# Routing the last token tile by column halves, with a centred router, in a fused perceiver and mixture-of-experts kernel

## The chip, the cores and the metric

The kernel runs on one core of one Trainium2 chip. The metric is the device time of one execution in microseconds (us). Four engines compute: TensorE (PE, matrix products; its weight loads are listed as PEld), VectorE (DVE), ScalarE (ACT) and GpSimd (POOL). SyncE (SP) only issues transfers. Each engine works through its own instructions in order and waits on semaphores that the others raise.

## The reference

Everything is float32, and 512 tokens (8 x 64) of width 512 pass through three blocks, each with a residual. A cross attention over 1601 context rows and a linear attention with its MLP come first. The third block, a mixture of eight experts, is where the change lies:

```python
x = x + _L0_xattn_ref(_layernorm(x), ctx_1024, W, b)
x = x + _L0_attn_ref(_layernorm(x), ...)          # ends with + gelu(h2 @ w1 + b1) @ w2 + b2
m = _layernorm(x).reshape(-1, 512)                # 512 tokens
router_logits = m @ w_router                      # 512 x 8
top_w, top_i = top_k(router_logits, 2)
top_w = softmax(top_w)
for ei in range(8):
    out = out + gating[:, ei:ei+1] * ((silu(m @ w0[ei]) * (m @ w1[ei])) @ wo[ei])
x = x + out
```

This layernorm has no scale or shift of its own. So a logit is (x - mean) @ w_router divided by the token's standard deviation.

## The kernel before, in words

**Tiles.** The 512 tokens are NT = 4 tiles of 128. The width of 512 is KC = 4 chunks of 128. The instructions of each engine stand in the order in which the code writes them (a manual schedule), and waits are put in from the data flow. PSUM is eight banks: four under the tag `mm` and four under `acc`, each handed out in turn.

**End of the MLP.** `mlp_out(t, f, hid)` (L808) adds the product of hidden chunk f with `w2` to the bank `acc[t]`. The last HELD = 8 of the 16 hidden chunks are held back, and `last_chunks(t, part)` plays them tile by tile. A float32 product is two passes of TensorE, so a profile counts two instructions for each. `finish(t)` then adds the bank to the residual `xs` on DVE (L844), takes the mean and variance (L846, L848), the square root on ACT (L850), the reciprocal (L851), and writes the normalized tile `mn` (L852). ACT's queue stores `mn` to DRAM (L855), POOL's queue stores `xs` to the output (L856).

**Routing of a tile**, placed between the last chunks of the next tile:

- `turn_m(t)` transposes `mn` on PE (L867) and ACT copies the result to `m_t` (L869).
- `route(t)` multiplies with the router on PE (L875), copies the logits (L879), takes the two largest and their places (L880, L882), casts the places to floats as `chosen` (L883), and forms `hot` and `member` (L884, L890).
- `rank_tile(t)` counts on PE how many earlier tokens chose each expert (L904 with `members`, L905 with `member`); DVE makes `rank` (L906) and the one-hot matrix of the places in expert 0's list (L910).
- `first_rows(t)` (L915) multiplies `mn` with that matrix into one bank: the transposed rows of expert 0's first 128 tokens, gathered without going through DRAM.
- `count_tile(t)` updates `members` (L894, L896). `tabulate(t)` (L929 to L944) computes where each token goes in a table in DRAM, and POOL scatters two columns there with indirect transfers.

After the last tile, `xgT_first` is copied out of the bank (L975), the counts per expert are made (L982, L984) and so are the gating weights: L987, an exponential on ACT (L988), L990 to L997, and a store on ACT's queue (L998). POOL reads the table back as `late` (L1000).

**Experts.** `whole_tile` runs an expert's first 128 tokens: four `up` products (L1097), Silu on ACT (L1060), a product on DVE (L1062), a transpose on PE (`ht`, L1068), and the `y` products (L1105). Expert 0 reads `xgT_first`. The other experts' rows are fetched by indirect transfers through `late` (L1033) and transposed (L1051). An expert with 129 to 160 tokens runs `group` too (L1135 on), and one with over 160 runs `big_tile`s of 128 rows at the end. The buffers of this part reuse the memory of the part before it, so some of its first instructions also wait for the old part's transfers.

**Weights** come through a ring of twelve 1 MB buffers, issued by SP (L192) in a fixed order, each as soon as its buffer is free.

Of the kernel before, what the change touches and what calls it, by code (L numbers as in the profile page):

```python
# [15 lines left out]
F32 = mybir.dt.float32  # L16
AF = mybir.ActivationFunctionType
# [29 lines left out]
def perceiver_kernel(  # L47
# [189 lines left out]
    for e in range(NE):  # L237
# [16 lines left out]
    slot = const.tile([P, P], F32, name="slot")  # L254
    nc.gpsimd.iota(
        slot, pattern=[[1, P]], base=1, channel_multiplier=0, allow_small_or_imprecise_dtypes=True
    )
    token = const.tile([P, NT], F32, name="token")
    nc.gpsimd.iota(
# [142 lines left out]
    def late_loads():  # L402
        nc.sync.dma_start(out[B * S :, :], zero[:, :D])
        nc.sync.dma_start(table.rearrange("p k two -> p (k two)"), zero[:, : NE * NI * 2])
        nc.sync.dma_start(b2_bc, b2.partition_broadcast(P))
        for r in range(2):
            nc.sync.dma_start(proj2[r * DH : (r + 1) * DH, :], proj)
# [120 lines left out]
    def values(t, n):  # L528
# [5 lines left out]
            )  # L534
        nc.scalar.copy(v_sb[:, t, n * 512 : (n + 1) * 512], bank)

    for g in range(4):
        key_group(0, g)
    for g in range(2):
        key_group(1, g)  # L540
    for t in range(NT):
        turn_scores(t)
        if t == NT - 1:

            nc.scalar.activation(warm0, eps, AF.Sqrt)
        if t > 0:
            add_and_normalize(t - 1)
        weigh(t, 0)
        key_group(t + 1, 2)
        if 0 < t < NT - 1:  # L550
            turn_h(t - 1)
        weigh(t, 1)
        if t == NT - 1:
            turn_h(t - 1)
        key_group(t + 1, 3)
        weigh(t, 2)
        if t == NT - 3:
            late_loads()

        if t < NT - 2:  # L560
            key_group(t + 2, 0)
        else:
            values(t - 2, 0)
        turn_av(t)
        if t < NT - 2:
            key_group(t + 2, 1)
        else:
            values(t - 2, 1)
        attended(t)
# [269 lines left out]
    member = moe.tile(full, F32, name="member")  # L839
    members = moe.tile(full, F32, name="members")  # L840

    def finish(t):

        nc.vector.tensor_tensor(xs[:, t, :], acc[t], xs[:, t, :], ALU.add)  # L844
        st = small.tile([P, 6], F32, tag="st", name=f"st_m_{t}")
        nc.vector.bn_stats(st, xs[:, t, :])  # L846
        mv = small.tile([P, 2], F32, tag="mv1", name=f"mv_m_{t}")
        nc.vector.bn_aggr(mv, st)  # L848
        rstd = small.tile([P, 1], F32, tag="rstd1", name=f"rstd_m_{t}")
        nc.scalar.activation(rstd, mv[:, 1:2], AF.Sqrt, bias=eps)  # L850
        nc.vector.reciprocal(rstd, rstd)  # L851
        nc.vector.tensor_scalar(  # L852
            mn[:, t, :D], xs[:, t, :], mv[:, 0:1], rstd, ALU.subtract, ALU.mult
        )
        nc.scalar.dma_start(mn_dram[t * P : (t + 1) * P, :D], mn[:, t, :D])  # L855
        nc.gpsimd.dma_start(out[t * P : (t + 1) * P, :], xs[:, t, :])  # L856

# [1 line left out]
        for f in part:  # L859
            mlp_out(t, nf - HELD + f, hids[nf - HELD + f])  # L860

    m_ts = {}

    def turn_m(t):
        bank = mm_bank(f"tr_m_{t}")
        for c in range(KC):
            nc.tensor.transpose(bank[:, c * P : (c + 1) * P], mn[:, t, c * P : (c + 1) * P], ident)  # L867
        m_ts[t] = mlp2.tile([P, KC, P], F32, tag="mT", name=f"m_t_{t}")
        nc.scalar.copy(m_ts[t].rearrange("p c q -> p (c q)"), bank)  # L869

    def route(t):

        bank = mm_bank(f"router_{t}")
        for c in range(KC):
            nc.tensor.matmul(  # L875
                bank[:, :NE], m_ts[t][:, c, :], router[:, c, :], start=(c == 0), stop=(c == KC - 1)
            )
        logits = small.tile([P, NE], F32, tag="logits", name=f"logits_{t}")
        nc.vector.tensor_copy(logits, bank[:, :NE])  # L879
        nc.vector.max(out=top[:, t, :], in_=logits)  # L880
        where = small.tile([P, NE], mybir.dt.uint32, tag="where", name=f"where_{t}")
        nc.vector.max_index(out=where, in_max=top[:, t, :], in_values=logits)  # L882
        nc.vector.tensor_copy(chosen[:, t, :], where[:, :2])  # L883
        nc.vector.tensor_tensor(  # L884
            hot[:, t, :, :],
            enum[:, None, :].to_broadcast([P, 2, NE]),
            chosen[:, t, :, None].to_broadcast([P, 2, NE]),
            ALU.is_equal,
        )
        nc.vector.tensor_tensor(member[:, t, :], hot[:, t, 0, :], hot[:, t, 1, :], ALU.add)  # L890

    def count_tile(t):
        if t == 0:
            nc.vector.tensor_copy(members[:, 0, :], member[:, 0, :])  # L894
        else:
            nc.vector.tensor_tensor(members[:, t, :], members[:, t - 1, :], member[:, t, :], ALU.add)  # L896

    onehots = {}

    def rank_tile(t):  # L900

        bank = mm_bank(f"rank_{t}")
        if t > 0:
            nc.tensor.matmul(bank[:, :NE], ones, members[:, t - 1, :], start=True, stop=False)  # L904
        nc.tensor.matmul(bank[:, :NE], earlier, member[:, t, :], start=(t == 0), stop=True)  # L905
        nc.vector.scalar_tensor_tensor(  # L906
            rank[:, t, :], bank[:, :NE], 1.0, member[:, t, :], ALU.add, ALU.mult
        )
        onehots[t] = mlp2.tile([P, P], F32, tag="onehot", name=f"onehot_{t}")
        nc.vector.tensor_scalar(onehots[t], slot[:, :P], rank[:, t, 0:1], None, ALU.is_equal)  # L910

    def first_rows(t):

        for c in range(KC):
            nc.tensor.matmul(  # L915
                first_bank[:, c * P : (c + 1) * P],
                mn[:, t, c * P : (c + 1) * P],
                onehots[t],
                start=(t == 0 and c == 0),
                stop=(t == NT - 1),  # L920
                skip_group_check=True,
            )

    def tabulate(t):

# [26 lines left out]

    last_chunks(0, range(HELD))
    finish(0)
    first_bank = acc_bank("first_rows")
    for t in range(1, NT):

        last_chunks(t, range(0, 4))
        turn_m(t - 1)
        last_chunks(t, range(4, 5))  # L960
        route(t - 1)
        last_chunks(t, range(5, 7))
        rank_tile(t - 1)
        last_chunks(t, range(7, HELD))
        finish(t)
        first_rows(t - 1)
        if t > 1:
            tabulate(t - 2)
        count_tile(t - 1)
    turn_m(NT - 1)  # L970
    route(NT - 1)
    rank_tile(NT - 1)
    first_rows(NT - 1)
    xg_t0 = moe.tile([P, KC, P], F32, name="xgT_first")
    nc.scalar.copy(xg_t0.rearrange("p c q -> p (c q)"), first_bank)  # L975
    count_tile(NT - 1)
    for t in range(NT - 2, NT):
        tabulate(t)


    bank = mm_bank("counts")
    nc.tensor.matmul(bank[:, :NE], ones, members[:, NT - 1, :], start=True, stop=True)  # L982
    count = moe.tile([P, NE], F32, name="count")
    nc.vector.tensor_copy(count, bank[:, :NE])  # L984

    e2 = moe.tile([P, NT], F32, name="e2")
    nc.vector.tensor_tensor(e2, top[:, :, 1], top[:, :, 0], ALU.subtract)  # L987
    nc.scalar.activation(e2, e2, AF.Exp)  # L988
    r1 = moe.tile([P, NT], F32, name="r1")
    nc.vector.tensor_scalar_add(r1, e2, 1.0)  # L990
# [17 lines left out]
    if True:  # L1008
# [36 lines left out]
        def turn_tile(key, n=P):  # L1045

            xg = fetched[key]
            name = f"xgt_{key[0]}_{key[1]}"
            bank = (y_bank("w", name) if n == P else side_bank(1, name))
            for c in range(KC):  # L1050
                nc.tensor.transpose(  # L1051
                    bank[:, c * n : (c + 1) * n], xg[:n, c * P : (c + 1) * P], ident[:n, :n]
                )
            xg_t = moe2.tile([P, KC, n], F32, tag=f"xgT{n}", name=f"xgT_{key[0]}_{key[1]}")
            evacuate(xg_t.rearrange("p c q -> p (c q)"), bank[:, : KC * n])
            turned[key] = xg_t

        def gated(side, bank, name):
            act = moe2.tile([P, FQ], F32, tag=f"act{side}", name=f"act_{name}")
# [28 lines left out]
        def whole_tile(key, up_of, down_of, between=lambda k: None):  # L1088
# [5 lines left out]
            def up(q):  # L1094
                bank = side_bank(0, f"up_{nm}_{q}")
                for c in range(KC):
                    nc.tensor.matmul(  # L1097
                        bank, xg_t[:, c, :], up_of[q][:, c, :], start=(c == 0), stop=(c == KC - 1)
                    )
                return gated(0, bank, f"{nm}_{q}")  # L1100

# [25 lines left out]
        def group(e, up_of, down_of):  # L1127
# [5 lines left out]
            for c in range(KC):  # L1133
                for q in range(NQ):
                    nc.tensor.matmul(  # L1135
                        bank[q * R : (q + 1) * R, :],
                        xg_t[:, c, :],
                        up_of[q][:, c, :],
                        start=(c == 0),
                        stop=(c == KC - 1),  # L1140
                    )
# [17 lines left out]
        if True:  # L1159
# [135 lines left out]
                    [tiles["wo", n] for n in range(2)],  # L1295
                )

            turned[0, 0] = xg_t0
            for e in range(NE):

                def between(k, e=e):
# [126 lines left out]
```

## Time and profile before

| | us |
|---|---|
| three runs of the kernel before | 671.36, 673.45, 673.49 (median 673.45) |
| the profiled execution's own time | 672.11 |
| its span, first to last instruction | 670.4 |
| PE busy in the span | 627.2 (94%) |
| DVE, ACT, POOL busy | 175.5, 128.3, 61.6 |
| mean granted TensorE clock | 0.981 |

Times below are us from the start of the profiled span. A matmul's start is well placed; its end is modelled, so starts are compared with starts. "PEclk" is the share of full speed that the TensorE clock had.

### The profile page before, as it was taken

What the parts mean: (1) busy time and instruction counts of PE and PEld (TensorE: products, weight loads), DVE (VectorE), ACT (ScalarE), POOL (GpSimd) and SP (SyncE); (2) the same over time, 40 slices, a digit from 0 to 9 for tenths busy, and PEclk for the clock granted to TensorE, in tenths of its full rate; (3) what the DMA queues carried; (4) which work ended last, traced back from release to release, by engine and by line L of the source; (5) the groups of instructions that cost most, each with busy time, mean ns of one, the idle gap of its engine ahead of it and who ended that gap; (6) DMA issues with size and microseconds to landing.
All of it is one profiled execution on the core that took longest, in us unless ns stands there. A gap on an engine that the chain in (4) does not pass through costs nothing. (4 is left out here: it accounts for less than half of the span.)

```text
span 670.4 us, 6808 instructions
## 1 busy us (share of the span) xinstructions
PE 627.2 (94%) x2664; PEld 291.2 (43%) x2664; DVE 175.5 (26%) x419; ACT 128.3 (19%) x240; POOL 61.6 (9%) x81
## 2 busy tenths in 40 slices
PE   4998989799999999999999998899999899999993
PEld 3743434243444444454444455433444344334441
DVE  4011323122316888650000045311210111100100
ACT  2241222220132223031011211211111211111110
POOL 2000000000000000060000001340202202210000
PEclk9998999899999999999999999799999999999997
DMA  8999999999421203030213115029389576694611
GB/s 326 420 420 389 420 384 418 374 386 413 194 111 43 85 1 127 1 126 18 107 64 125 63 64 188 3 69 350 137 314 337 176 314 229 205 359 177 269 16 19
DMA packets 24224, 138.08 MB, mean 206 GB/s; under 512 B 4164, under 2 KB 4164, under 8 KB 11896
## 3 DMA queue, kind: packets, MB, share of 16 engines
q1 hardware_dynamic: 20056, 129.90, 49.7%
q0 software_dynamic: 3024, 6.58, 4.4%
q10 hardware_dynamic: 1104, 1.07, 0.5%
q8 instruction: 25, 0.41, 0.2%
q14 instruction: 15, 0.12, 0.1%
HBM read 132.56 MB, written 4.97 MB: 205 GB/s over the span
## 5 line engine op out<-in xcount | busy, mean ns | idle before, releaser
L1097 PE MATMUL up<-e_up,xgT 128*128 128x512 f32 x224 | 100.2, 595 | 1.2 <-PEq L1326 1.2
L1097 PEld LDWEIGHTS up<-e_up,xgT 128*128 128x128 f32 x224 | 40.9, 190 | 50.4 <-issue 50.4
L1105 PE MATMUL y<-e_wo,hidT 128*128 128x512 f32 x128 | 61.0, 599 | 0.0
L808 PE MATMUL mlp<-w,hid_sb 128*128 128x512 f32 x128 | 58.8, 597 | 0.0
L1062 DVE TENSOR_TENSOR mid<-up,act 128x256 f32<-128x256 f32 x35 | 14.9, 425 | 162.4 <-ACT act L1060 162.4
L472 PE MATMUL av<-ctx,eT 128*64 128x512 f32 x192 | 50.2, 636 | 7.3 <-DMA ctx<-in_ctx_dram 6.5
L787 PE MATMUL hid<-v_sb,w 128*128 128x512 f32 (+2 forms) x144 | 56.6, 545 | 0.0
L423 PE MATMUL sc<-ctxT,pw_t 128*64 128x401 f32 (+1 forms) x256 | 48.1, 501 | 0.6 <-DMA ctxT<-in_ctx_T_dram 0.6
L787 PEld LDWEIGHTS hid<-v_sb,w 128*128 128x128 f32 x144 | 26.2, 190 | 29.1 <-issue 27.3
L808 PEld LDWEIGHTS mlp<-w,hid_sb 128*128 128x128 f32 x128 | 23.4, 190 | 24.9 <-issue 24.9
L1060 ACT ACTIVATE act<-up 128x256 f32<-128x256 f32 x35 | 13.4, 384 | 104.5 <-PE up L1097 95.6
L1078 POOL DMA_INDIRECT out_dram<-y_sb,dst_late x11 | 16.8, 1530 | 160.9 <-ACTq L1326 103.7
L423 PEld LDWEIGHTS sc<-ctxT,pw_t 128*64 128x64 f32 x256 | 20.2, 136 | 26.0 <-issue 22.6
L802 POOL TENSOR_TENSOR xin<-xin,b_bc 128x512 f32<-128x512 f32 x4 | 5.1, 1269 | 283.4 <-DVE rstd_h L744 279.1
L1105 PEld LDWEIGHTS y<-e_wo,hidT 128*128 128x128 f32 x128 | 22.4, 190 | 19.5 <-issue 19.1
L472 PEld LDWEIGHTS av<-ctx,eT 128*64 128x64 f32 x192 | 15.2, 143 | 35.8 <-issue 24.3
L706 PE MATMUL wo<-wo,a_t 128*128 128x512 f32 x64 | 29.1, 600 | 0.5 <-DVE a_t L682 0.5
L595 PE MATMUL wk<-h_t,wk 128*128 128x512 f32 x64 | 29.5, 604 | 0.0
L595 PE MATMUL wq<-h_t,wq 128*128 128x512 f32 x64 | 29.4, 602 | 0.0
L532 PE MATMUL v<-wv,h_t 128*128 128x512 f32 x64 | 28.7, 597 | 0.6 <-DVE h_t L519 0.6
L680 DVE RECIPROCAL rden<-rden 128x512 f32<-128x512 f32 x8 | 26.8, 3353 | 0.3
L844 DVE TENSOR_TENSOR xs<-mlp,xs 128x512 f32<-128x512 f32 x4 | 2.8, 691 | 87.3 <-PE mlp L808 87.3
(229 smaller groups left out, 630.0 us busy)
## 6 DMA issues: line engine op xcount, KB each, us to landing
e_up<-in_L_ffn_up_dram SPq DMA_DIRECT2D x32, 1024.0 KB, 7.8
ctx<-in_ctx_dram SPq DMA_DIRECT2D x24, 1024.0 KB, 17.4
ctxT<-in_ctx_T_dram SPq DMA_DIRECT2D x24, 802.0 KB, 15.7
e_wo<-in_L_ffn_wo_dram SPq DMA_DIRECT2D x16, 1024.0 KB, 11.3
w<-in_L_attn_w_dram SPq DMA_DIRECT2D x8, 1024.0 KB, 10.9
ctxT<-in_ctx_T_dram SPq DMA_DIRECT2D x8, 796.0 KB, 16.7
big_up<-in_L_ffn_up_dram SPq DMA_DIRECT2D x4, 1024.0 KB, 7.9
wv<-in_L_attn_wv_dram SPq DMA_DIRECT2D x2, 1024.0 KB, 13.1
```

What stands on the lines that cost most here:

```text
L423: nc.tensor.matmul(sc[h * S : (h + 1) * S, :width], pw_t[:, c, (2 * t + h) * S : (2 * t + h + 1) * S], keys[h][:, c, :], start=(c == 0), s ...
L472: nc.tensor.matmul(av[h * S : (h + 1) * S, :], e_t[:, 4 * g + j, h * S : (h + 1) * S], rows[h][:, j, :], start=(g == 0 and j == 0), stop=F ...
L532: nc.tensor.matmul(bank, h_t[:, c, t * P : (t + 1) * P], wv_n[:, c, :], start=(c == 0), stop=(c == KC - 1))
L595: nc.tensor.matmul(bank, w[:, c, (j % 4) * P : (j % 4 + 1) * P], h_t[:, c, :], start=(c == 0), stop=(c == KC - 1),)
L680: nc.vector.reciprocal(rden, rden)
L706: nc.tensor.matmul(wo_banks[t], a_t[:, j, t * P : (t + 1) * P], wo_r[j // 4][:, j % 4, :], start=(j == 0), stop=(j == nj - 1),)
L787: nc.tensor.matmul(hid_banks[f][:, tokens], w[:, c, (f % 4) * P : (f % 4 + 1) * P], h2_t[:, c, tokens], start=(c == 0), stop=(c == KC - 1),)
L808: nc.tensor.matmul(acc[t], hid[:, t * P : (t + 1) * P], need("w2", f // 4)[:, f % 4, :], start=(f == 0), stop=(f == FF // P - 1),)
L1062: nc.vector.tensor_tensor(hid, bank[:, FQ:], act, ALU.mult)
L1078: nc.gpsimd.indirect_dma_start(out=out, out_offset=bass.IndirectOffsetOnAxis(ap=dst[:n, :], axis=0), in_=y_sb[:n, :], in_offset=None, boun ...
L1097: nc.tensor.matmul(bank, xg_t[:, c, :], up_of[q][:, c, :], start=(c == 0), stop=(c == KC - 1))
L1105: nc.tensor.matmul(y, h_t[:, j, :], w[:, 2 * (q % 2) + j, :], start=(q + j == 0), stop=(q + j == NQ))
```

## The change

The router's columns are centred once: the mean over the 512 rows is subtracted from each (`centre_router`, in the cross-attention stage). Then `xs @ router_c` is the logit times the token's standard deviation. The order of a token's logits is the same, so routing works on `xs` as it stands, ahead of the statistics. The difference of the two largest is multiplied by the reciprocal deviation later.

The last tile's held products are computed in two column halves, the second in a bank of its own. Tile 2's routing goes between the pieces of both halves, and so do the transposes and logits of the first half of tile 3. The gathering products `first_rows`, which had followed each tile, are all moved to the end, in portions that stand between the steps of the last tile's routing. They go to two banks that ACT and DVE copy out side by side. The logits are read from PSUM, and the places are compared without the cast in between. `rank` is off the one-hot's way, the counts are copied directly after the gathered rows, `tabulate` of tiles 0 and 1 comes one tile earlier, and tile 3's `mn` is made on ACT, its two stores issued after the counts. The diff, cut to its core:

```diff
+    router_c = const.tile([P, KC, NE], F32, name="router_c")
+    def centre_router():                       # called in the attention loop at t == NT - 3
+        bank = mm_bank("router_sums")
+        for c in range(KC):
+            nc.tensor.matmul(bank[:, :NE], ones, router[:, c, :], start=(c == 0), stop=(c == KC - 1))
+        nc.vector.scalar_tensor_tensor(
+            router_c, bank[:, None, :NE].to_broadcast([P, KC, NE]), -1.0 / D, router, ALU.mult, ALU.add)
...
-            nc.tensor.transpose(bank[:, c * P : (c + 1) * P], mn[:, t, c * P : (c + 1) * P], ident)
+            nc.tensor.transpose(bank[:, i * P : (i + 1) * P], xs[:, t, c * P : (c + 1) * P], ident)
...
-        nc.vector.tensor_copy(logits, bank[:, :NE])
+        logits = route_banks[t][:, :NE]
...
-        nc.vector.tensor_copy(chosen[:, t, :], where[:, :2])
...
+        onehots[t] = mlp2.tile([P, P], F32, tag="onehot", bufs=NT, name=f"onehot_{t}")
+        nc.vector.tensor_scalar(
+            onehots[t], slot0, bank[:, 0:1], member[:, t, 0:1], ALU.is_equal, ALU.mult
+        )
         nc.vector.scalar_tensor_tensor(
             rank[:, t, :], bank[:, :NE], 1.0, member[:, t, :], ALU.add, ALU.mult
         )
-        onehots[t] = mlp2.tile([P, P], F32, tag="onehot", name=f"onehot_{t}")
-        nc.vector.tensor_scalar(onehots[t], slot[:, :P], rank[:, t, 0:1], None, ALU.is_equal)
...
-    for t in range(1, NT):
-        last_chunks(t, range(0, 4))
+    for t in range(1, NT - 1):
+        last_chunks(t, range(0, 3))
         turn_m(t - 1)
-        last_chunks(t, range(4, 5))
-        route(t - 1)
+        rank_before(t - 1)
+        last_chunks(t, range(3, 5))
+        logits_of(t - 1)
+        choose(t - 1)
         last_chunks(t, range(5, 7))
         rank_tile(t - 1)
+        count_tile(t - 1)
         last_chunks(t, range(7, HELD))
         finish(t)
-        first_rows(t - 1)
-        if t > 1:
-            tabulate(t - 2)
-        count_tile(t - 1)
-    turn_m(NT - 1)
-    route(NT - 1)
-    rank_tile(NT - 1)
-    first_rows(NT - 1)
-    nc.scalar.copy(xg_t0.rearrange("p c q -> p (c q)"), first_bank)
-    count_tile(NT - 1)
+        tabulate(t - 1)
+    t = NT - 1
+    first_banks = [acc_bank(f"first_rows_{h}") for h in range(2)]
+    second_bank = acc_bank("mlp_second")
+    half_chunks(0, range(0, 5))              # 256 columns of the held products of tile 3
+    turn_m(t - 1)
+    rank_before(t - 1)
+    half_chunks(0, range(5, HELD))
+    for h in range(2):
+        nc.vector.tensor_tensor(xs[:, t, halves[h]], acc[t][:, halves[h]], xs[:, t, halves[h]], ALU.add)
+    logits_of(t - 1)
+    choose(t - 1)
+    half_chunks(1, range(0, 3))
+    turn_m(t, range(0, 2))
+    nc.vector.bn_stats(st[:, 0, :], xs[:, t, halves[0]])
+    half_chunks(1, range(3, 5))
+    rank_tile(t - 1)
+    count_tile(t - 1)
+    half_chunks(1, range(5, 7))
+    logits_of(t, range(0, 2))
+    rank_before(t)
+    half_chunks(1, range(7, HELD))
+    nc.vector.tensor_tensor(xs[:, t, halves[1]], second_bank[:, :HD], xs[:, t, halves[1]], ALU.add)
+    first_rows(4)
+    turn_m(t, range(2, KC))
+    nc.vector.bn_stats(st[:, 1, :], xs[:, t, halves[1]])
+    mv, rstd = moments(t, st)                # aggregate, square root on ACT, reciprocal
+    nc.vector.scalar_tensor_tensor(neg_mean, mv[:, 0:1], -1.0, rstd, ALU.mult, ALU.mult)
+    nc.scalar.activation(mn[:, t, :D], xs[:, t, :], AF.Identity, bias=neg_mean, scale=rstd)
+    first_rows(2)
+    logits_of(t, range(2, KC))
+    choose(t)
+    first_rows(5)
+    rank_tile(t)
+    first_rows(1)
+    count_tile(t)
+    first_rows(KC)
+    bank = mm_bank("counts")
+    nc.tensor.matmul(bank[:, :NE], ones, members[:, NT - 1, :], start=True, stop=True)
+    for h, copy in enumerate([nc.scalar.copy, nc.vector.tensor_copy]):
+        copy(xg_t0[h].rearrange("p c q -> p (c q)"), first_banks[h][:, : 2 * P])
+    nc.vector.tensor_copy(count, bank[:, :NE])
+    write(NT - 1)                            # the two stores of tile 3
     for t in range(NT - 2, NT):
         tabulate(t)
...
     nc.vector.tensor_tensor(e2, top[:, :, 1], top[:, :, 0], ALU.subtract)
+    nc.vector.tensor_tensor(e2, e2, rstds, ALU.mult)
     nc.scalar.activation(e2, e2, AF.Exp)
```

`first_rows(n)` now plays the next n of the sixteen products (tile t = i // 4, chunk c = i % 4). `rank_before(t)` is the L904 half of the ranking, and `logits_of` and `choose` are the two parts of `route`.

## The prediction

> **What bounds the kernel now.** I read the page first: PE is busy for 94% of the span, so only time that PE loses counts. The list of PE's waits after 424 us then shows none on a transfer, so what is gained before the experts should reach the end. The timeline of PE around the change shows the gap (columns: start, duration, engine, line, operation, count, idle time before and what ended it):
>
> ```profile
> 411.40 1.10 PE L808 MATMUL mlp<-w,hid_sb 128*128 128x512 f32 x2
> 412.34 1.05 PE L915 MATMUL first_rows<-onehot,mn 128*128 128x128 f32 x8
> 415.41 0.66 PE L867 MATMUL tr_m<-ident,mn 128*128 128x128 f32 x4 [2.02 <-DVE mn L852]
> 416.79 1.88 PE L875 MATMUL router<-col,m_t 128*128 128x8 f32 x8 [0.73 <-ACT m_t L869]
> 418.52 0.57 PE L904 MATMUL rank<-members,ones 128*128 128x8 f32 x2
> 420.02 0.59 PE L905 MATMUL rank<-member,earlier 128*128 128x8 f32 x2 [0.93 <-DVE member L890]
> 421.20 2.08 PE L915 MATMUL first_rows<-onehot,mn 128*128 128x128 f32 x8 [0.58 <-DVE onehot L910]
> 423.07 0.43 PE L982 MATMUL counts<-members,ones 128*128 128x8 f32 x2
> 423.95 1.22 PE L1097 MATMUL up<-e_up,xgT_first 128*128 128x512 f32 x1 [0.45 <-ACT xgT_first L975]
> ```
>
> After the last held product (next start 412.34) PE does little until `up` starts at 423.95: one tile's routing runs as a chain over four engines. The table by stretches shows the second loss (stretch, length, PE busy, granted clock, DMA share, GB/s):
>
> ```profile
> 413.35:416.76 3.41, 0.70 (x5) 1.00 0.88 293
> 416.76:420.17 3.41, 2.45 (x11) 0.50 0.45 171
> 420.17:423.59 3.42, 2.75 (x12) 0.50 0.02 3
> 423.59:427.00 3.41, 3.05 (x4) 0.50 0.01 0
> 427.00:430.41 3.41, 3.41 (x9) 1.00 0.08 5
> 635.21:638.62 3.41, 2.42 (x9) 1.00 0.01 2
> ```
>
> After a stretch in which PE was busy for 0.70 us the clock is halved for 10.2 us, into the first `up` products. Then ACT's timeline:
>
> ```profile
> 423.31 0.59 ACT L975 COPY xgT_first<-first_rows 128x512 f32<-128x512 f32 x1 [6.57 <-PE first_rows L915]
> 423.92 1.28 ACT L988 ACT_TABLE_LOAD   x1
> 425.21 0.20 ACT L988 ACTIVATE e<-e 128x4 f32<-128x4 f32 x1
> 426.52 0.38 ACTq L998 DMA_DIRECT2D mn_dram<-mn  x1
> 429.30 1.28 ACT L1060 ACT_TABLE_LOAD   x1 [3.88 <-PE up L1097]
> 430.59 0.38 ACT L1060 ACTIVATE act<-up 128x256 f32<-128x256 f32 x1
> ```
>
> In the built program the first Silu of expert 0 also waits for the landing of the gating store (L998), because the new buffers lie over the old `mn`. Here that is hidden: issued at 426.52, landed at 428.30 (its semaphore), and ACT waited for PE until 429.30.
>
> **The change part by part.** I count r from the start of the first PE instruction after tile 2's last product: 402.66 in this trace. In the kernel before, tile 3's products end at r 9.68, `up` starts at r 21.29, and the first transpose of expert 0 (`ht`) at 432.42, r 29.76.
>
> Rates at full clock, from PE's rows: a pass of 512 columns every 0.429 us, 256 columns every 0.216 (L368), 128 columns 0.112 (L915: 403.441 - 402.661 over 7), a router or rank pass 0.112, a transpose 0.108. PE to DVE takes about 0.2 us (409.20 to 409.41), a dependent step on DVE 0.2.
>
> *Tile 1.* `first_rows(0)` leaves the place after tile 1: 8 passes, 393.04 to 393.93, 0.89 us earlier for everything after. The work comes back at the end, below.
>
> *PE until the last held product.* Halves 0 to 4: 10 x 0.216 = 2.16; transposes 0.44; rank 0.22; three halves 1.30; router 0.92 (r 5.04); three 1.30; two transposes 0.22; two halves 0.86; rank 0.22; two 0.86; half of tile 3's logits 0.45; rank 0.22; the last 0.43. Sum: r 9.61. Does a wait come in? DVE has finished tile 2 and `tabulate(1)` at r 4.2 (402.93 to 406.9 here), adds the halves from 4.4 to 5.2, chooses from 5.28 to 6.14 (0.86; here 1.26 with the two copies L879 and L883, 0.2 each); the rank asks at 7.42. `members` is ready at 8.45, asked for at 8.95. So no, with 0.5 us to spare.
>
> *The tail.* DVE adds half 1, r 9.88 to 10.30. PE has `first_rows(4)`, to 10.51, transposes to 10.73, two products to 11.18. ACT copies 256 columns, 10.99 to 11.38. PE's logits 11.43 to 11.88. DVE chooses 12.15 to 13.01, behind the reciprocal and `neg_mean`, which wait for ACT's square root behind that copy. PE's five products end at 13.0; rank 13.05 to 13.27; one product; one-hot 13.45 to 13.74; the last four 13.78 to 14.68 (`mn` from ACT is ready at 12.74). Copies: ACT 14.43 to 14.80, DVE 14.88 to 15.29, counts to 15.49. The program lets `up` wait for that last copy, which holds the bank, not just for its data. So `up` starts at r 15.55: **5.74 us** earlier than 21.29.
>
> *First products to `ht`.* At full clock `up(0)` and `up(1)` take 16 x 0.429 = 6.87 instead of 8.47, so `ht` could come at r 22.4. But the gating chain is later: the counts are copied ahead of both `tabulate`s (1.23 us each, 421.14 to 422.37 to 423.60). From r 15.49: tables to 17.9, difference and the added product 0.35, exponential to 18.5, L990 to L997 to 19.57 (1.07 here), store issued 19.61 and landed 1.78 later, 21.4. Then the Silu table 1.28, Silu 0.38, the product 0.42, and steps between: `ht` at r 23.65. PE stalls 1.2 us where it had none; 29.76 - 23.65 = 6.11, of which 5.74 are counted: **0.37**. Behind the waiting Silu, ACT holds nothing that is due.
>
> [...] The row gives 1.28 us for the table load, and Silu starts 0.01 us after it (429.30 + 1.28, 430.59). [...]
>
> *The clock.* In this trace the clock fell after stretches with PE busy 0.70 us of 3.41 (and 1.03 at 58.36, 1.06 at 126.63), and held with 2.42. In the new tail PE idles about 1.3 us of 5.9, and in the stall 1.2, so it should hold. [...] The longest gap here is 2.02 us and it fell. [...] by the row, a poor window is enough, so the new tail is not out of danger. [...] the row gives the first rival.
>
> *Transfers.* Tile 3's `mn` store (ACT's queue) moves from 415.38 to about r 15, behind a copy; it delays the exponential's table load by 0.35, which still ends at 16.5, before it is needed. Its `xs` store on POOL's queue stays ahead of the scatters of tile 2, and those of tiles 0 and 1 run a tile earlier. So the scatters of tile 2 start when their places are ready, r 16.75, instead of at 424.43 (r 21.77), where the earlier scatter held them. From there to reading the table back takes 10.09 (to 434.52), so `late` comes 5.0 us earlier and PE's first use of a fetched row (444.89) about 6.1. The fetch was issued 6.45 us before that use and lands in 2.7 at best; a margin shrinks by 1.1, no stall. SP's last two loads of expert 1 wait for `w2` to be released, 2 us later at most, and are used after 457: nothing.
>
> *Centring.* Eight passes more, 0.9 us of PE near 106 us, plus a small product on DVE. In that stage PE later waits 2.65 us for context rows (128.98), which could absorb it all; if the loads are held by buffers that PE frees, it costs 0.9. I take **-0.4**. The extra iota on POOL (0.24 for its twin L255) lies at 3 us, ahead of idle time: nothing, and at most 0.24 without that.
>
> Sum: 0.89 + 5.74 + 0.37 - 0.4 = **6.6 us**. Against the profiled execution (672.11: span 670.4 and 1.7 around it) that is 665.5. The median of the runs is 673.45, which gives 666.9; I say 666.2, between.
>
> **The rivals.**
> - *The tail throttles* (15%). Small products and short gaps leave a window poor. Against it: busy shares near 80%. Price: the work after r 11, 3.5 us of PE time at most, doubled, and `up(0)` 1.7 slower of which 1.2 fills the stall. Gain 2.5 to 5: about 669.
> - *The gating store is late* (14%). PE's new stall lengthens one for one. The store of tile 3's `mn` took 4.1 us to land at 415.38 beside weight loads; [...] For it: the first `ht` now hangs on ACT and DVE. Against: DMA is at 0.01 to 0.08 there. Gain 4.3 to 5.2: 668.
> - *A router decision flips* (2%), which ends slower. The reference gives the experts 133, 104, 217, 159, 87, 132, 70 and 122 tokens, so expert 3 stands one token under 161. Rounding in the uncentred products would have to move one token to it; then its group (9.3 us, as the one from 581.06 to 590.33) becomes a second big tile, of about 24 us as the first (635.97 to about 660): +14 - 6.6, about 680. Against: the closest second and third logits differ by 0.0014 at a spread of 1.47.
> - *It does not do what it says* (4%): a bank or semaphore serializes the pieces, and the tail stays as long as it was: 672.
>
> **How the numbers follow.** The forecast has 65%, with its own range 664.5 to 668.5 (centring between 0 and -0.9, runs 2.1 us apart). With the two milder rivals the range is 664 to 670. A measurement of this kernel tells about 0.3% (2 us) from no change. Faster by more: the first three cases less 0.02 for their edges, 0.92; within: the last case and an edge, 0.05; slower: the flip and an edge, 0.03.
>
> **What would show it.** Right: no `first_rows` between tiles; PE's clock 1.00 through the tail; from tile 2's last product to `up` about 15.6 us; a stall of about 1.2 us before the first `ht`, ended by DVE's `mid` and behind it by the gating store. Wrong: half clock there, a stall over 3 us, PE waiting for fetched rows, or a fourth group or second big tile.

## The result, and the profile after

| | before | after |
|---|---|---|
| median of 5 runs, us | 673.45 (671.36 to 673.82) | 663.46 (662.06 to 665.04) |
| profiled execution's own time | 672.11 | 665.04 |
| its span | 670.4 | 663.3 |
| PE busy in the span | 627.2 | 624.8 |
| mean granted clock | 0.981 | 0.987 |

The ratio is 0.9856, with a 95% interval of 0.9835 to 0.9876. The change makes the kernel 10 us faster by these medians, and 7.1 us by the two traces. The profiled execution of before was among the faster of its runs, that of after the slowest of its five. In later runs the changed kernel had a median of 665.37 (662.93 to 665.68, 4 runs; ratio 0.9872, 0.9855 to 0.9889). All ten runs of it, in the order of size, are 662.06, 662.29, 662.93, 663.46, 663.69, 664.95, 665.04, 665.21, 665.54 and 665.68: a median of 664.3. The kernel before had medians of 673.1 to 673.5 in every set. So the gain is nearer 8.9 us than 10.

PE's timeline after, at the same place (start, duration, engine, line, operation, count, idle time before and its releaser):

```profile
410.75 0.68 PE L1033 MATMUL mlp_second<-w,hid_sb 128*128 128x256 f32 x2
411.27 1.05 PE L969 MATMUL first_rows<-onehot,mn 128*128 128x128 f32 x8
412.16 0.38 PE L901 MATMUL tr_m<-ident,xs 128*128 128x128 f32 x2
412.38 0.61 PE L969 MATMUL first_rows<-onehot,mn 128*128 128x128 f32 x4
413.00 0.61 PE L913 MATMUL router<-router_c,m_t 128*128 128x8 f32 x4
413.47 1.36 PE L969 MATMUL first_rows<-onehot,mn 128*128 128x128 f32 x10
414.67 0.29 PE L953 MATMUL rank<-member,earlier 128*128 128x8 f32 x2
414.81 0.47 PE L969 MATMUL first_rows<-onehot,mn 128*128 128x128 f32 x2
415.49 1.13 PE L969 MATMUL first_rows<-onehot,mn 128*128 128x128 f32 x8 [0.21 <-DVE onehot L955]
416.46 0.29 PE L1077 MATMUL counts<-members,ones 128*128 128x8 f32 x2
417.26 7.11 PE L1200 MATMUL up<-e_up,xgT_first 128*128 128x512 f32 x16 [0.51 <-issue]
425.29 0.44 PE L1171 MATMUL ht<-ident,mid 128*128 128x128 f32 x2 [0.93 <-DVE mid L1165]
```

The gathering products stand between the steps of the last routing, and PE's waits of 2.02, 0.73, 0.93 and 0.58 us have gone. What remains is 0.21, 0.51 and a new wait of 0.93 ahead of `ht`. The next table goes by stretches of 3.41 us, which I call clock windows: in these traces the clock is halved for 3.41, 6.83, 10.24 or 13.65 us at a time, until the last 9 us of the span. Its columns are stretch, length, PE busy (instructions), granted clock, DMA share and GB/s:

```profile
410.15:413.57 3.42, 3.40 (x28) 1.00 0.88 348
413.57:416.98 3.41, 2.96 (x25) 1.00 0.88 329
416.98:420.39 3.41, 3.13 (x8) 1.00 0.21 77
...
423.81:427.22 3.41, 2.48 (x8) 1.00 0.03 5
```

No window has PE busy for less than 2.48 us, and the clock is never halved here. ACT's timeline shows what stands behind the new wait:

```profile
419.94 0.20 ACT L1091 ACTIVATE e<-e 128x4 f32<-128x4 f32 x1 [2.02 <-DVE e L1090]
421.24 0.38 ACTq L1101 DMA_DIRECT2D mn_dram<-mn  x1
423.10 1.28 ACT L1163 ACT_TABLE_LOAD   x1 [2.96 <-DMA mn_dram<-mn]
424.40 0.66 ACT L1163 ACTIVATE act<-up 128x256 f32<-128x256 f32 x2
```

Silu's table load waits for the landing of the gating store. Silu starts 1.30 us after the load's start. From `ht` to the end of the span it is 238.0 us in both traces, so nothing of the gain is given back behind it.

### The profile page after: what moved, and what is told of

It is laid out like the page before. It is cut to its first block, busy times and chain, and to the rows that moved or that the text cites. A ratio compares the mean times of both kernels' runs of the same rounds, so it can differ in the third digit from the quotient of the medians.

```text
span 663.3 us, 6862 instructions
## 1 busy us (share of the span) xinstructions
PE 624.8 (94%) x2688; PEld 292.5 (44%) x2688; DVE 175.4 (26%) x421; ACT 128.9 (19%) x242; POOL 61.8 (9%) x82
## 5 line engine op out<-in xcount | busy, mean ns | idle before, releaser
L830 PE MATMUL mlp<-w,hid_sb 128*128 128x512 f32 x112 | 51.0, 597 | 0.0
L428 PE MATMUL sc<-ctxT,pw_t 128*64 128x401 f32 (+1 forms) x256 | 46.6, 501 | 0.0
L1181 POOL DMA_INDIRECT out_dram<-y_sb,dst_late x11 | 16.8, 1530 | 159.9 <-ACTq L1429 103.7
L830 PEld LDWEIGHTS mlp<-w,hid_sb 128*128 128x128 f32 x112 | 20.7, 190 | 23.5 <-issue 23.4
```

The costliest lines, as they stand in the source:

```text
L428: nc.tensor.matmul(sc[h * S : (h + 1) * S, :width], pw_t[:, c, (2 * t + h) * S : (2 * t + h + 1) * S], keys[h][:, c, :], start=(c == 0), s ...
L830: nc.tensor.matmul(acc[t], hid[:, t * P : (t + 1) * P], need("w2", f // 4)[:, f % 4, :], start=(f == 0), stop=(f == FF // P - 1),)
L1181: nc.gpsimd.indirect_dma_start(out=out, out_offset=bass.IndirectOffsetOnAxis(ap=dst[:n, :], axis=0), in_=y_sb[:n, :], in_offset=None, boun ...
```

## The experiments

I compare traces mostly from a fixed point: the first product of `v` after the cross attention, which in both recorded traces starts at 135.11. From there to `ht` is 297.31 us before (432.42) and 290.18 after (425.29). What happens ahead of `v`, with the clock or with the context transfers, is then out of the comparison.

### The unchanged kernel as a measure

> The kernel before, unchanged, for more runs with their granted clocks and a second trace. The pair of traces so far differs by 7.1 us (670.4 to 663.3 of span) and is identical to 0.01 us at the first value product (135.11) and the first hidden product (294.0); the medians differ by 10.0. Theory 'spread': the runs differ in how long the clock is halved somewhere, and the first trace of before was a lucky one: times between 671 and 674 whose order follows the clock (0.981 in the first trace, about 0.977 at 674), and a trace that shows where the further halved 3.4 us windows lie. Rival 'nothing to do with the clock': times spread as before at one and the same clock, and the stage that differs is the context stage before 135 us, bound by transfers.

The ratio is 1.0 (0.9991 to 1.0009), with a median of 673.08. Its trace has a span of 671.2, `v` at 135.91, and 297.27 us from there to `ht`. The tail repeats; the stage before `v` came out 0.8 us later. The theory of this run, that the time follows the granted clock, does not hold for this kernel: runs of it with a clock of 0.982 took from 671.25 to 673.60 us.

### Filling PE's gaps in the old tail

```diff
+    def fill(name, widths):
+        bank = mm_bank(f"fill_{name}")
+        for n in widths:
+            nc.tensor.matmul(bank[:, :n], ones, mn[:, 0, :n], start=True, stop=True)
...
+    fill("turn", [512, 512])      # and 256, 384, 256 columns: ahead of the logits, in the ranking, ahead of the gathered rows
```

> The kernel before with products that nobody reads put into PE's gaps of the last tile's routing: two of 512 columns ahead of the transposes, one of 256 ahead of the logits, one of 384 inside the ranking, one of 256 ahead of the gathered rows. No link of the chain is shortened. Theory 'chain': the clock stays at 1.00, so what was run at half speed gets faster: logits 0.95, ranking 0.5, gathered rows 1.0, first up products 1.6, less 0.3 of overhang: 3.5 to 4 us faster, and the other half of the change's gain is the shorter chain. Rival 'clock alone': 6 us or more, nearly all that the change gave. Rival 'latency alone': under 1.5 us, as the fillers only take the place of idle time. If the length of the halved stretch is what makes the runs of before differ, this kernel's runs lie closer together than those of before and its gain in the medians is above that in the traces.

The median is 669.48 (ratio 0.9961, 0.9948 to 0.9975). From `v` to `ht` it takes 294.73 us, 2.6 less than before. The windows of the tail:

```profile
415.35:418.77 3.42, 3.01 (x18) 1.00 0.81 299
418.77:422.18 3.41, 2.29 (x15) 1.00 0.02 3
```

The clock stays full in this trace, although no useful work was moved. So the half clock is a loss of its own. Filling won 2.6 of the 7.1 us here, where I had expected 3.5 to 4; the other 4.5 came with the new order. It didn't bring all that the half clock had taken: `up` came only 1.05 us earlier from `v` (287.79 against 288.84), and PE is idle for 1.27 us ahead of it. In that time ACT copies the gathered rows, and DVE copies the counts at 422.61, behind the tabulation of an earlier tile; I take it that this copy holds `up` back, as the counts' bank did in the working of the prediction. (In the last version below, PE's wait before `up`, 0.44 us, is put down to the copy of the counts.)

The runs show more than the trace. Nine of the fifteen had a granted clock of 0.990 to 0.993 and took 667.78 to 669.84 us; six had 0.982 to 0.987 and took 670.92 to 672.74. None of the six was traced, so it is not shown where their clock was lost, and it is not shown that this filling keeps the clock in every run.

### Eight of the sixteen gathering products back ahead of the last tile

```diff
     st = small.tile([P, 2, 6], F32, tag="st2", name="st_m_last")
+    first_rows(8)
     half_chunks(0, range(0, 5))
...
-    first_rows(2)
...
-    first_rows(5)
...
-    first_rows(1)
```

> The changed kernel with eight of the twelve waiting gathering products put ahead of tile 3's held products, so that the steps of the last routing have only four products beside them. The work moved is 8 x 0.224 = 1.8 us of PE. Theory 'chain': at least 1.8 us slower; and the columns that PE streams between the last held product and the up products fall to about 30% of the time, [...]so it is halved again: about 1.5 us more in the tail and up to 0.5 in the first up products beyond the stall: 3 to 4 us slower, half clock in the trace. [...] Rival 'the filled tail is PE-bound': no slower or under 1 us, because the tail gets shorter by what is moved.

The windows of this tail, where PE's longest gap is 0.95 us:

```profile
409.67:413.08 3.41, 2.54 (x19) 1.00 1.00 392
413.08:416.50 3.42, 1.83 (x13) 1.00 0.83 302
416.50:419.91 3.41, 3.41 (x5) 0.50 0.11 38
```

With the filling gone, a window has 1.83 us of PE work, and the clock is halved for one window, just when `up` starts. From `v` to `ht` it takes 292.49 us, 2.3 more than the changed kernel. The median, 664.99 (ratio 0.989, 0.987 to 0.9911), does not stand apart from the changed kernel's; in the profiled run the context stage came 2.65 us earlier (`v` at 132.46), which hides the 2.3. My 3 to 4 us were too many: only one window is halved, not three.

### The last tile in whole passes

```diff
-    half_chunks(0, range(0, 5))
+    last_chunks(t, range(0, 3))
     turn_m(t - 1)
...
-    for h in range(2):
-        nc.vector.tensor_tensor(xs[:, t, halves[h]], acc[t][:, halves[h]], xs[:, t, halves[h]], ALU.add)
...
+    nc.vector.tensor_tensor(xs[:, t, :], acc[t], xs[:, t, :], ALU.add)
     first_rows(4)
-    turn_m(t, range(2, KC))
+    turn_m(t)
```

> The changed kernel, but the last tile is formed in whole passes of 512 columns as before (no column halves, one add of 512 columns on DVE, all eight logit products behind it, both moments at the end), everything else as changed: centred router, eleven gathering products between, two banks, early count copy. Worked from the rows of the changed kernel: the held products end 0.67 us earlier [...], but the add then takes 512 columns, four transposes and all eight logits stand behind it, about 1.15 us more. Theory (the halves only shift work, the order of the gathering products is what fills PE): about 0.5 us slower than the changed kernel, clock still full in the tail. Rival (the halves are the main part of the gain): 2 us slower or more, with half clock back in the tail.

The timeline of PE:

```profile
410.22 1.05 PE L969 MATMUL first_rows<-onehot,mn 128*128 128x128 f32 x8
...
412.62 1.06 PE L913 MATMUL router<-router_c,m_t 128*128 128x8 f32 x8 [0.28 <-ACT m_t L904]
...
417.32 7.11 PE L1181 MATMUL up<-e_up,xgT_first 128*128 128x512 f32 x16 [0.51 <-issue]
```

The held products end 1.05 us earlier than with halves, and `up` starts 0.06 later. From `v` to `ht`: 290.32 against 290.18. The median is 663.6 (ratio 0.9865, 0.9848 to 0.9882). So the column halves, which the change is named after, are worth about 0.1 us in these traces (I had expected 0.5); the rival that made them the main part has fallen. What PE does ahead of the last held product with the halves, it does behind it without them: two of the transposes, half of the logits and a rank pass, by the rates of the prediction 0.9 of the 1.05 us.

### The gating factors in a buffer of their own

```diff
-    gating = mn[:, :, D:]
+    gating = moe.tile(full, F32, name="gating")
```

> The changed kernel with the gating weights in a buffer of their own instead of the last columns of mn, so the first Silu of expert 0 no longer waits for the landing of the gating store; nothing else is changed. Theory 'gating store': the stall of 0.93 us before the first transpose of expert 0 (PE idle there, about 1.2 us in starts) is gone, that transpose comes 1.1 to 1.2 us earlier relative to the first up product (6.9 us instead of 8.0), and the whole kernel is 1.0 to 1.2 us faster than the changed one, 11 us faster than before. [...] Rival 'given back': the fetched rows come no earlier, and PE waits for them instead, so the total is the same.

The median is 662.93 (ratio 0.9843, 0.9825 to 0.9861). ACT's timeline:

```profile
421.15 0.38 ACTq L1101 DMA_DIRECT2D mn_dram<-gating  x1
421.77 1.28 ACT L1163 ACT_TABLE_LOAD   x1 [1.71 <-DVE few_i L1277]
423.06 0.38 ACT L1163 ACTIVATE act<-up 128x256 f32<-128x256 f32 x1
```

The table load no longer waits for the store. `ht` follows `v` after 289.09 us, 1.09 less (1.1 to 1.2 were expected), and PE has no stall ahead of it. The wait behind the new stall is thereby shown to be the store's.

### What the centring products do where they stand

Before the next three runs I knew that the medians differed by more than the traces, and that the kernels with the change often had an earlier context stage. First, the centred router alone, in the kernel before, and unused:

```diff
             late_loads()
+            centre_router()
```

> The kernel before, plus the centred router computed in the context stage as the changed kernel does, and not used. What is open is why the medians differ by 9 to 10 us where the two traces differ by 7.1. Theory B (the eight products alter when PE idles in the context stage, and with it whether the clock is halved there at 127 to 133 us): 1 to 3 us faster than before in the median. Theory C (they cost and bring nothing; the rest is that runs of the kernel before lie tight whatever their clock, since the place of the clock's windows that helps one stage hurts the other): the same as before, within 0.5 us.

The median is 670.78 (ratio 0.9978, 0.9965 to 0.9991), and `v` starts at 133.49. This spoke for theory B. Then the changed kernel with the same call moved to the MLP:

```diff
             late_loads()
-            centre_router()
...
+    centre_router()
     last_chunks(0, range(HELD))
```

> The changed kernel with its eight centring products and the small DVE product moved from the context stage to just ahead of the held products of tile 0, where PE has no idle time. Theory B (the place in the context stage brings luck with the clock there): 0.9 us for the products that are now on PE's path and 1 to 2.7 us more, 665.5 to 667. Theory C: only the 0.9 us, about 664.3.

The median is 665.05 (ratio 0.9889, 0.9874 to 0.9905). That is between the two forecasts (C 664.3, B 665.5 to 667), and 0.75 us above the 664.3 of the changed kernel's ten runs. The trace decides for C, with the centring products now in the MLP:

```profile
135.11 1.13 PE L537 MATMUL v<-wv,h_t 128*128 128x512 f32 x2
...
377.67 0.95 PE L548 MATMUL router_sums<-col,ones 128*128 128x8 f32 x8
```

`v` starts at 135.11, as with the products in the context stage; from `v` to `ht` it takes 291.07, so 0.89 us more. On PE's path the products cost 0.89 us, and in the context stage nothing.

> The changed kernel unchanged, for a second trace. Both theories expect the tail as in the first trace (first products of expert 0 to start 15.6 us after the last product of tile 2, full clock); theory B expects that the half clock at 127 to 133 us is sometimes absent, with the following stage then about 2.7 us earlier.

A second trace of the changed kernel: its own time is 664.95, `v` at 135.02, 290.18 to `ht`, and the same 6.8 us of half clock at 126.6.

Neither theory explained why, even without the products, the last wait for context rows ended earlier in the changed kernels. The rows of PE in that stage, first of before and then of after:

```profile
128.98 4.92 PE L472 MATMUL av<-ctx,eT 128*64 128x512 f32 x13 [2.65 <-DMA ctx<-in_ctx_dram]
...
135.11 1.13 PE L532 MATMUL v<-wv,h_t 128*128 128x512 f32 x2
```

```profile
127.73 6.16 PE L477 MATMUL av<-ctx,eT 128*64 128x512 f32 x13 [2.66 <-DMA ctx<-in_ctx_dram]
...
135.11 1.13 PE L537 MATMUL v<-wv,h_t 128*128 128x512 f32 x2
```

The rows arrive 1.25 us earlier after the change. In this pair of traces nothing of it is left at `v`, because the clock was halved for two windows there (6.8 us from 126.85), and for one in the kernel before (3.4 us from 130.04).

### Where the tiles lie

In the built programs the context tiles and the weight ring begin at byte 32,128 of a partition before and at 32,768 after: `slot0` and `router_c` add 640 bytes of constants ahead of them. 32,128 is 128 past a multiple of 256, 32,768 is a multiple. So theory D: the place of the tiles decides. One unused constant moves them, with no instruction changed:

```diff
+    const.tile([P, 40], F32, name="spare")
     token = const.tile([P, NT], F32, name="token")
```

> The kernel before with one unused constant of 40 columns, which moves the context tiles and weight tiles from 384 bytes past a multiple of 512 in the SBUF partition (32,128) to a multiple of 512 (32,256), where the changed kernel's constants also put them (32,768); no instruction is added, taken away or moved. Theory D (where the tiles start sets the length of the context transfers): a 1024 KB context transfer takes 17.0 to 17.1 us instead of 17.4, PE's last wait for context rows ends at about 127.5 instead of 128.98, and the median falls by 1 to 2.4 us, as with the unused centred router (670.8). Theory B (the centring products themselves): nothing changes, 673.2, transfers 17.4.

The reverse, in the changed kernel, with 104 columns (and with 72 and 24 for the two traces after it, single runs of 664.2 and 665.15 us):

> The changed kernel with an unused constant that puts the context and weight tiles back to 384 bytes past a multiple of 512 (33,152), its centring products still in the context stage. Theory D: transfers of 17.4 us again, the last wait for context rows ends at about 129, and the median is 1 to 2.5 us above the changed kernel's, 664.5 to 666. Theory B: no change, 663.5.

> The changed kernel with the tiles at 256 bytes past a multiple of 512 (33,024). Theory D leaves open whether only the multiple of 512 counts (transfers of 17.4 us) or a multiple of 256 does as well (17.1); theory B expects 17.1.

> The changed kernel with the tiles at 64 bytes past a multiple of 512 (32,832). Theory D: if only the multiple of 512 counts, transfers of 17.4 us, as for 384; if 64 bytes are enough, 17.1. Theory B: 17.1.

PE's row for the last wait, in the kernel before with tiles at a multiple of 512, and in the changed kernel with tiles at 384:

```profile
127.66 3.22 PE L473 MATMUL av<-ctx,eT 128*64 128x512 f32 x13 [2.83 <-DMA ctx<-in_ctx_dram]
...
132.09 3.70 PE L533 MATMUL v<-wv,h_t 128*128 128x512 f32 x8
```

```profile
129.03 6.00 PE L478 MATMUL av<-ctx,eT 128*64 128x512 f32 x13 [2.75 <-DMA ctx<-in_ctx_dram]
```

The end of this wait moves with the address, in both kernels and both ways:

| start of the tiles, past a multiple of 512 bytes | end of PE's last wait for context rows, us |
|---|---|
| 0 (11 traces) | 127.36 to 128.16 |
| 256 (1 trace) | 127.93 |
| 64 (1 trace) | 128.91 |
| 384 (5 traces) | 128.56 to 129.24 |

So a multiple of 256 seems to be what counts here, and 512 not to be needed, on one trace each. It is worth 1.2 us on the arrival of the last rows (means of 127.8 and 128.9 for 0 and 384). In the runs less is left: 672.27 for the kernel before with the constant (ratio 0.9986, 0.9978 to 0.9994, so 0.4 to 1.5 us), and 664.94 for the changed kernel with tiles at 384 (ratio 0.9878, 0.9859 to 0.9896), which is not apart from the ten runs' 664.3. I had expected more of both. The unused centred router also moved the tiles of the kernel before to a multiple of 512 (its wait ended at 127.36). By its ratio it gained 0.6 to 2.4 us, an interval that overlaps with that of the constant, so no part of its gain is shown to be the products'. The median time of a 1024 KB context transfer moved as expected in these two runs (16.8 and 17.3 us), but in later traces it did not separate the cases (17.0 and 17.3 the other way round); the end of the wait did in all 18, by 0.4 us at the least.

### Two lengths of the old tail, and a last version

The trace of the kernel with the spare constant had another surprise: 298.61 us from `v` to `ht`, where the traces of before had 297.3. Its half clock in the tail lasted 13.7 us and not 10.2. Was that the price of its undisturbed context stage?

> The kernel before unchanged, for one more trace. Theory D: a 1024 KB context transfer takes 17.3 to 17.4 us and PE's last wait for context rows ends at about 129. Coupling (what a run gains with the clock in the context stage, its slow tail gives back): from the first product of v to the first transpose of expert 0 it takes 297.3 us where the context stage had a half clock, and over 298 where it had none. Without coupling: 297.3 in any case.

> The kernel before with the unused constant of 40 columns (tiles at a multiple of 512 bytes), for one more trace. Theory D: transfers of 16.8 to 17.1 us, the last wait ends at about 127.6. Coupling: 297.3 us from v to the first transpose of expert 0 with a half clock in the context stage, over 298 without; without coupling the first trace's 298.6 was chance and 297.3 comes in any case.

> The changed kernel unchanged, timed again in new rounds beside new runs of the kernel before. If the difference of the medians (10.0 us) over that of the two traces (7.1) was chance, the medians now differ by 7 to 8; if it is the place of the tiles and the clock in the context stage, by 9 to 10 again.

| trace with the old tail | half clock ahead of `v`, from 90 us on | half clock in the tail | `v` to `ht`, us |
|---|---|---|---|
| before | 3.4 | 10.2 from 416.8 | 297.31 |
| before again | 6.8 | 10.2 from 417.4 | 297.27 |
| before, centred router unused | 3.4 | 10.2 from 415.3 | 297.38 |
| before, spare constant | none | 13.7 from 412.6 | 298.61 |
| before, spare constant, second trace | 3.4 | 13.7 from 414.6 | 298.63 |
| before, third trace | 6.8 (two separate windows) | 13.7 from 415.7 | 298.80 |

The coupling has fallen as I put it: two traces have both a half clock ahead of `v` and the long tail. What shows is that the old tail has two lengths, 297.3 and 298.7. They go with the place of the window: counted from the first PE instruction after tile 3's held products, the clock falls after 4.3 to 4.6 us in the three short tails and after 3.3 to 3.8 in the three long ones. No run sets that place, so this is a regularity of six traces. The windows of the unchanged kernel in its third trace:

```profile
412.28:415.70 3.42, 1.36 (x11) 1.00 0.71 235
415.70:419.11 3.41, 2.31 (x10) 0.50 0.60 229
419.11:422.52 3.41, 2.09 (x9) 0.50 0.02 3
422.52:425.94 3.42, 2.97 (x8) 0.50 0.01 0
425.94:429.35 3.41, 3.41 (x5) 0.50 0.08 5
429.35:432.76 3.41, 3.41 (x9) 1.00 0.01 0
```

Here one of the halved windows holds 2.09 us of PE work (2.75 in the recorded trace of before), and the clock comes back one window later. The changed kernel has one length: 290.18 in its first two traces, 290.20 in the third, and 290.18 with the tiles at 384, 256 and 64.

The medians of the changed kernel's later runs and of before differ by 8.0 us. That is the branch for which the 10.0 of the first runs were in part chance, and not the one of 9 to 10 again.

The last version has the gating factors in their own buffer and the counts copied by ACT:

```diff
-    nc.vector.tensor_copy(count, bank[:, :NE])
+    nc.scalar.copy(count, bank[:, :NE])
...
-    gating = mn[:, :, D:]
+    gating = moe.tile(full, F32, name="gating")
```

> The changed kernel with the gating factors in a buffer of their own (so the first Silu doesn't wait for their store) and the copy of the counts on ACT instead of DVE. From the traces: the first takes the stall of 0.9 us and some of the steps out of the way between the first products of expert 0 and their transpose (1.1 to 1.2 us, as with the own buffer alone), the second lets these products start 0.2 us earlier, since ACT is done 0.45 us before DVE. 1.3 us together, about 662.2; if the copy on ACT takes as long as it gains, 662.4 to 662.9 as with the own buffer alone.

The median is 662.51 (660.58 to 664.55; ratio 0.9844, 0.9826 to 0.9862). `ht` follows `v` after 289.04, so the copy on ACT adds nothing to the own buffer's 289.09: `up` starts 282.10 after `v` instead of 282.15. Its profiled execution shows what a run can be when no window is halved between 16 and 651 us: a span of 658.8. Both versions with the own buffer are 1.1 us ahead of the changed kernel in the traces; their intervals overlap with its own.

## Why the prediction was right and wrong

**The chain through the tail was right.** With r from the first PE instruction after tile 2's last product (401.60 in this trace), tile 3's products end at r 9.67, `up` starts at 15.66, the gating store is issued at 19.64, and `ht` comes at 23.69. Each is within 0.12 us of the working. The stall is 0.93 us instead of 1.2, with the store behind it. The clock holds (1.00 in every window from 410.15 to 427.22), and nothing is given back: the two spans differ by 7.1 us, of which 6.1 lie in the tail and 1.06 before it, where I had 0.89 for tile 1 (the other 0.17 was not traced). The first rival, a throttled tail, has no half clock to show. The second, a late store, did not come either: the table load that waits for it starts 1.86 us after its issue, and 1.78 were reckoned to its landing. No router decision flipped, and the pieces do what they say.

**The rows held for the table load and the clock.** Silu starts 1.30 us after the start of its table load, on the path of PE, so the load cost no more there than the 1.28 us of its row. Nor did the fall of the clock take a long gap: with eight gathering products ahead of the tile it fell after a window with PE busy for 1.83 us and no gap above 0.95, and in the kernel before the longest gap was 2.02.

**The term that failed first is the centring, -0.4.** I let eight products cost PE up to 0.9 us. In the context stage they cost 0.0 (`v` at 135.11 with and without). What was left out is the other thing that centring and `slot0` bring: 640 bytes, which move every context tile to a multiple of 256. That brings the rows 1.2 us earlier, and it brought the runs of the kernel before 0.4 to 1.5; in the changed kernel, putting the tiles back made no difference that stands apart. The diff shows two new constants; I asked only what they cost to make, and put their effect on the addresses at nothing without a reason. The table above goes with a step of 256 (0 and 256 early, 64 and 384 late; 256 and 64 on one trace each). The address that moved is the one that the transfers write to; why it counts, no run shows.

**The second is the base.** The sum was set against one execution, with the old tail in its short form. In three of six traces that tail is 1.4 us longer, so against the kernel's runs the tail is worth 7.1 or 8.5 us, 7.8 in the mean of the six traces, where I had 7.0 without the centring. With 0.9 for the place of the tiles that is an estimate of 8.7, against 8.9 between the ten runs and before.

**The third is the range.** Its low end, 664.0, allowed for runs 2.1 us apart and for no gain that I had not named. The recorded median, 663.46, is 0.54 below it; the ten runs' 664.3 would be inside. The changed kernel's runs lie 3.6 us apart and those of before 3.1, and with four or five runs a median moves by more than 1 us (663.46 and 665.37). So that the result fell below the range, and not just inside it, is in part chance. The spread of the changed kernel goes with its granted clock: the five runs at 0.986 and 0.987 took 664.95 to 665.68 us, the five at 0.988 to 0.993 took 662.06 to 663.69. Where in the run the clock differs stays open: all three of its traces, with two halved windows just ahead of `v`, are of the first five.

## What to carry to other kernels

Fill a stretch of dependent small steps with work that has to be done anyway: here the waits of 2.02, 0.73, 0.93 and 0.58 us went and the clock stayed at 1.00, where it had been 0.50 for 10.2 us, while the finer column halves brought 0.1 us. When a change adds or removes a buffer, see where the large tiles behind it now start, and cost that as a part of the change: here it moved the end of a stage by 1.2 us. Where one trace has a half clock, take a second one before using its length as the base of a sum: here it was 10.2 us in three traces and 13.7 in three.

## What the hardware did that I had not expected

- The clock fell after windows of 3.41 us with PE busy for 1.83 (eight gathering products ahead), 1.40, 1.39 and 1.36 us (the long tails). The busy time alone does not tell when: it held after 1.81 in the kernel before (from 450.89) and after 1.50 in the last version (from 125.47). The window's place against the program differs from run to run, so the same code loses three windows (10.2 us) in one run and four (13.7 us) in another.
- The starting address of the 1 MB tiles in their partitions moved the end of a stage that waits for transfers by 1.2 us (127.8 against 128.9), with no instruction changed.
- A table load on the path cost its 1.28 us and nothing more: Silu started 0.02 us after its end (423.10 + 1.28, 424.40).
